# Decay factors of a selective scan in two sets of tiles, one bank of PSUM and two tiles of SBUF each, written two rounds ahead

## The chip, the core and the metric

The kernel runs on one core of a Trainium2 chip. The metric is the device time of one execution in microseconds: 8020.21 us, the median of three runs (8017.12 to 8021.32). The profile is of one further execution.

## What is computed

The reference is a small hybrid network on images of 56 x 56 positions and 96 channels, in float32, four of them in a batch: two state-space blocks, each with a selective scan in four directions, and then two layers of linear attention with a quantised feed-forward net. The two scans take nearly all of the time. Cut to what matters here, one direction of one image is

```
dt  = softplus(dt_raw @ dtw.T + dtb)                 # 192 channels, 3136 positions
d_a = exp(dt[..., None] * a)                         # 192 channels x 16 states
d_b = dt[..., None] * b_ssm[:, None, :]
h_t = d_a_t * h_(t-1) + d_b_t * x_t                  # the recurrence over positions
y_t = sum over states of h_t * c_t
```

In this text d_a is called the decay, d_b times x the product, and the sum over states is y. There are 2 blocks x 4 images x 4 directions = 32 such scans.

## The kernel before

The 3136 positions of a direction are cut into 7 steps of 448 (`CS`). The 192 x 16 pairs of channel and state of one step are cut into 8 rounds: two halves of the channels (e) and four groups of states (q). A round has 3 groups (g) of 128 partitions, each partition one pair of channel and state. So there are 32 x 7 x 8 = 1792 rounds.

The engines take a round between them as follows; the lines are those of the profile.

- TensorE spreads the round's rows of B over 128 partitions into the PSUM tile b (line 616, `spread_b`, called from `begin`).
- ScalarE writes the three decays of the round, exp of dt times a, to the tiles da0, da1 and da2 (line 678, `decay`).
- VectorE multiplies du (dt times the input) by b for g = 0 and 1 (line 719, `products`), into the tile h. GpSimd does the same for g = 2 from its own copy of B in SBUF, cb (line 714).
- VectorE runs the recurrence of each g in place in h with the decay tile as the factor (line 726, `scan`).
- GpSimd multiplies the three groups of h by C, also in cb, into hc (line 768).
- Two rounds later TensorE sums hc over the states into the PSUM tile y (line 799), and ScalarE moves y out after each fourth round (line 806).

Before, da0 to da2 are three PSUM tiles of one bank each, with a single set: the decay of round n+1 is written to a tile as soon as the scan of round n has read it. [...]

A step is prepared over the rounds ahead of it, at offsets o counted in rounds from its first round: parameters and inputs (o = -14 and -12), projection on TensorE into pp (-12, -11), its rows to cf on ScalarE and the removal of the upper bits (-10 to -8), the step size dt with softplus (-8 to -6), the product du on GpSimd (line 521, o = -5), writing both to DRAM and reading them back spread over the partitions (lines 526 and 532, o = -5 to 0), and one read of cb for each q (line 550, o = -3 to 0). All these transfers are issued by SyncE's queue (SP).

Beside the scans, the other layers (`load`, `middle`, `branch`, `fuse`, `attend`) run as lanes: generators that give their instructions piece by piece at two places of a round, "F" (after the products) and "C" (between the scans of g = 0 and g = 1), while a budget of ScalarE and TensorE time (`spend`, `half_round`, `room`) lets them. Within the scan phase the order of the instructions on TensorE, ScalarE, VectorE and GpSimd is the order in which this program writes them, and each engine takes them in that order. `keep_busy` adds matmuls with zeros where TensorE would have little work in a round. After the last round, `late` gives the PSUM banks of the scans to the remaining lanes.

In the lanes, the convolution is done with matmuls by diagonal weights (dg), built by GpSimd (line 932, 27 small instructions) when the first image reaches it. Windows of the image for it lie in `win` with `NWIN` buffers.

Of the kernel before, what the change touches and what calls it, by code (L numbers as in the profile page):

```python
# [11 lines left out]
F32 = mybir.dt.float32  # L12
# [3 lines left out]
AF = mybir.ActivationFunctionType  # L16
ALU = mybir.AluOpType
# [5 lines left out]
C = 96  # L23
# [3 lines left out]
NG = 3  # L27
NQ = 4
NT = 112
CW = 448  # L30
# [6 lines left out]
NCS = L // CS  # L37
RANK = (12, 6)
NW, LATE_NW = 13, 20
NWIN = 5  # L40
OWN = ()
OWN_TAIL = ()

# [124 lines left out]
class Net:  # L168
    def __init__(self, ctx, tc, aps, at, out):
        self.tc, self.nc, self.aps, self.at, self.out = tc, tc.nc, aps, at, out  # L170
        pool = lambda name, **kw: ctx.enter_context(tc.tile_pool(name=name, **kw))
        self.const = pool("const", bufs=1)
        self.big = pool("big", bufs=1)
        self.psum = pool("psum", bufs=1, space=bass.MemoryType.PSUM)
        self.dram = pool("dram", bufs=1, space=bass.MemoryType.DRAM)
        self.nw, self.nwin, self.depth, self.banks, self.ring = NW, NWIN, DEPTH, BANKS, None
        self.tables = False
        self.both = self.big.tile([C, NE, L], F32, name="U")
        self.U = [self.both[:, e] for e in range(NE)]
        self.Y = [self.big.tile([C, L], F32, name=f"Y{e}") for e in range(NE)]  # L180
        self.wp = pool("work", bufs=2)
        self.setup()
        self.dg = None
        self.kept = (0, 0, 0)
        self.ready, self.loaded = set(), set()
        self.live, self.g = [], {}
        self.backlog, self.paced = [0.0, 0.0], False
        self.work = 0.0
        self.pool = pool
        d = lambda name, *shape: [self.dram.tile(list(shape), F32, name=f"{name}{i}") for i in range(NB)]  # L190
        self.ud, self.zd, self.yd, self.xrd = d("u", DI, L), d("z", DI, L), d("y", DI, L), d("xr", C, L)
        self.fd = d("f", C, L)
        self.xw, self.mw = d("x", C, L + 2 * HS), d("m", DI, L + 2 * HS)
        self.xd, self.md = [[t[:, HS : HS + L] for t in a] for a in (self.xw, self.mw)]
# [6 lines left out]
    def late(self):  # L201

        self.scan_pool.close()
        self.wp = self.pool("late", bufs=2)
        self.nw, self.nwin, self.depth, self.banks = LATE_NW, LATE_DEPTH + 1, LATE_DEPTH, LATE_BANKS
        tags = (("ps", BANKS), ("da0", 1), ("da1", 1), ("da2", 1), ("pp", 1), ("b", 1), ("y", 1))
        self.ring = cycle([t for t in tags for _ in range(t[1])])

    def ps(self):
# [345 lines left out]
    def prepare(self, ch, o):  # L555

        nc = self.nc
        if o == -14:  # L560
            self.parameters(ch)
        if o == (-14 if ch.opening else -12):
            self.inputs(ch)
        if o == -9:
            ch.cd = self.dram.tile([2 * NS, CS], F32, tag="cd", name="cd", bufs=3)
            nc.sync.dma_start(ch.cd, ch.cf[: 2 * NS])
        elif o == -5:
            self.times_u(ch)
            ch.dtd = self.park(ch.dtc)
        elif o == -4:  # L570
            ch.dud = self.park(ch.duc)
            self.spread_dt(ch, 0)
        elif o == -3:
            self.spread_du(ch, 0)
        elif o == 0:
            self.spread_du(ch, 1)
            self.spread_dt(ch, 1)
        if -3 <= o <= 0:
            self.fetch(ch, o + 3)

    def prepare_on_scalar(self, ch, o):

        if o == -10:
            self.rows(ch)
        elif o in (-9, -8):
            part = slice(64 if o == -9 else 96, 128)
            self.nc.scalar.copy(ch.cf[part], ch.ps[part])  # L587
        elif o in (-7, -6):
            self.softplus(ch, o + 7)

    def on_tensor(self, ch, o):

        for e in self.projected(ch, o):
            self.project_step(ch, e)
        if o in (-10, -9):
            self.less(ch, 64 if o == -10 else 96)
        elif o in (-8, -7):
            self.step_size(ch, o + 8)

    def projected(self, ch, o):  # L600

        return () if o not in (-12, -11) else (o + 12,) if not ch.first else (0, 1) if o == -11 else ()

    def less(self, ch, at):

# [6 lines left out]

    def spread_b(self, ch, q):

        ps = self.psum.tile([128, 512], F32, tag="b", name="b", bufs=1)[:, :CS]
        self.nc.tensor.matmul(ps, self.sel[:, q], self.upper(ch.cf), start=True, stop=True)  # L616
        return ps

# [4 lines left out]
    def scans(self):  # L623
# [24 lines left out]
        per = NE * NQ  # L648


        da = [self.psum.tile([128, 512], F32, name=f"da{g}")[:, : CS + 4] for g in range(NG)]
        for t in da:
            nc.vector.memset(t, 0.0)

        def steps(n):
# [4 lines left out]
            for ch, o in steps(n):  # L660
                self.on_tensor(ch, o)

        for n in range(-14, 0):
            for ch, o in steps(n):
                self.prepare(ch, o)
            if n > -8:
                yield "F", n, 0
            for ch, o in steps(n):
                self.prepare_on_scalar(ch, o)
            ahead(n)  # L670
            if n > -8:
                yield "C", n, 0

        def decay(n, g):

            if n < len(rounds):
                ch, e, q = rounds[n]
                nc.scalar.activation(da[g][:, INNER], ch.dt[e][:, g], AF.Exp, scale=ch.par.na[:, e, q, g : g + 1])  # L678

        def column(t, at):  # L680

# [39 lines left out]
        def scan(n, g):  # L721
            ch, e, q = rounds[n]
            c = 1 if ch.step else 0
            way = slice(CS + 1 + c, 1, -1) if ch.rev else slice(2 - c, CS + 2)
            h = hs[n][:, g * ROW :]
            nc.vector.tensor_tensor_scan(h[:, way], da[g][:, way], h[:, way], 0.0, ALU.mult, ALU.add)  # L726

        carried(0)
        carried(1)
        begin(0)  # L730
        self.exp_and_ln()
        self.tables = True
        for g in range(NG):
            decay(0, g)
        late = []
        for n, (ch, e, q) in enumerate(rounds):
            r = NQ * e + q
            products(n)
            for c, o in steps(n):
                self.prepare(c, o)  # L740
            self.half_round()
            strided = [1.5 + 1.5 * ch.orient] * (r % NQ == 2)
            strided += [1.5 + 1.5 * c.orient for c, o in steps(n) for _ in self.projected(c, o)]
            self.spend((0.6, 0.7, 1.7, 0, 0, 0, 0.7, 0.6)[r], (1.3, 1.3, 0, 0, 0, 0, 0.4, 0.4)[r] + sum(strided))
            yield "F", n, r
            for c, o in steps(n):
                self.prepare_on_scalar(c, o)
            ended = late.pop(0) if len(late) == 2 else None
            if ended:
                self.keep_busy(ended[2])  # L750
            begin(n + 1)
            if ended:
                self.add_up(*ended)
            ahead(n)
            self.half_round()
            for g in range(NG):
                if g == 1:
                    yield "C", n, r
                if g == 2 and ended and ended[2] == NQ - 1:
                    self.spend(0.6, 0)  # L760
                    self.keep_sums(*ended[:3])
                scan(n, g)
                if g == 2:
                    kept(n)
                decay(n + 1, g)
            carried(n + 2)
            hc = sp.tile([128, NG, CS], F32, name="hc", bufs=3)
            nc.gpsimd.tensor_tensor(  # L768
                hc, tokens(hs[n]), ch.cb[q][:, 0].unsqueeze(1).to_broadcast([128, NG, CS]), ALU.mult,
            )  # L770
            late.append((ch, e, q, hc))
            del hs[n], bs[n]
# [148 lines left out]
    def get(self, d, rows, s):  # L921
        t = self.w(rows)
        self.nc.sync.dma_start(t, d[:, s])
        return t

    def diagonals(self, w):

        t = self.wp.tile([C, 3 * NG, 3, 32], F32, name="dg", bufs=1)
        out = []
        for n in range(w.shape[1] // 3):  # L930
            for x in range(3):
                self.nc.gpsimd.tensor_scalar_mul(t[:, n, x], self.three, w[:, 3 * n + x : 3 * n + x + 1])
                yield "F0"
            out.append(t[:, n])
        return out

    def conv(self, diag, parts):
# [98 lines left out]
    def middle(self, i):  # L1036
# [49 lines left out]

        yield from self.overlap(part, NCW)

        if self.dg is None:
            self.dg = yield from self.run(self.diagonals(par("c96", "1conv_w")))  # L1090
        dg = self.dg

        def convolve(c):
# [212 lines left out]
    def gram(self, n, i, c, x, s):  # L1306

        nc = self.nc
        xr = self.wp.tile([C + 1, CW], F32, name="xra", bufs=self.depth)
        nc.scalar.activation(xr[C:], self.ident[C : C + 1, :1].to_broadcast([1, CW]), AF.Copy, scale=0.0, bias=1.0)  # L1310
        yield from self.normed(1e-5, x, 1, xr[:C])
        nc.sync.dma_start(self.xrd[i][:, s], xr[:C])
# [60 lines left out]
def tile_net(ctx: ExitStack, tc: tile.TileContext, aps, at, out):  # L1373
# [12 lines left out]
    lanes = alone([net.load(0)], lambda: "normed" in net.loaded)  # L1386
    net.fold_weights()
    net.open_scans()
    lanes = alone(lanes, lambda: 1 in net.loaded)

    beside = [
# [40 lines left out]
```

## Time and profile before

| | |
|---|---|
| median of 3 runs | 8020.21 us |
| profiled execution | 8016.8 us |
| its span | 8014.9 us |
| VectorE (DVE) busy | 7522.8 us, 94% |
| GpSimd (POOL) busy | 7170.8 us, 89% |
| TensorE (PE) busy | 7013.7 us, 88% |
| ScalarE (ACT) busy | 6114.5 us, 76% |
| first product to end of last scan | 87.17 to 7810.39 us |
| granted TensorE clock, mean | 0.907 |

A group of instructions is given as line, engine, operation, the tiles out<-in, the shape and the count, then the busy time in us and the mean of one in ns, then the idle time of that engine right before these instructions, and which instruction of another engine ended it. In a timeline the first two numbers are the start and the length in us; instructions of one kind that follow one another are merged (x2, x3). An engine that is blocked inside an instruction counts as busy.

### The profile page before, as it was taken

The page shows a single profiled execution, that of the slowest core. Times are in us where ns is not written, and L with a number is a line of the kernel's source. Part 1 is how long each engine was busy: PE and PEld are TensorE (multiplying, and loading weights), DVE is VectorE, ACT ScalarE, POOL GpSimd, SP SyncE. Part 2 cuts the span into 40 slices and gives each one's busy share as a digit, 9 for nine tenths or more (in the row PEclk, how much of TensorE's full clock was granted, in tenths as well). Part 3 has the DMA queues.
Part 4 walks back from the last instruction along what each step waited for, and adds up shares of the span by engine and source line. Part 5 has one row for each costly group of instructions (what it writes and reads, how often), then busy time and mean ns, then how long its engine had stood idle before and what let it go on. Part 6 is the DMA issues. An engine that isn't in the chain of part 4 may idle for free.

```text
span 8014.9 us, 113446 instructions
## 1 busy us (share of the span) xinstructions
PE 7013.7 (88%) x33765; PEld 2326.8 (29%) x33765; DVE 7522.8 (94%) x9600; ACT 6114.5 (76%) x12759; POOL 7170.8 (89%) x3989
## 2 busy tenths in 40 slices
PE   7888888889888988899889988988889888898888
PEld 3222222222222222222222223322233222332224
DVE  6999999999999999999999999999999999999992
ACT  6778878777778768887678876787877877678776
POOL 5999999999999999999989998999989999899990
PEclk8889989989899989999889999988999999998998
DMA  5556655557555665566655666555565555655552
GB/s 180 181 188 191 197 186 187 173 188 228 186 182 180 222 199 186 170 196 203 196 182 172 195 212 202 180 163 167 185 203 170 167 172 191 192 172 169 174 171 70
DMA packets 568239, 1467.53 MB, mean 183 GB/s; under 512 B 108034, under 2 KB 337156, under 8 KB 566756
## 3 DMA queue, kind: packets, MB, share of 16 engines
q1 hardware_dynamic: 566848, 1458.49, 57.0%
q8 instruction: 265, 4.34, 0.2%
q14 instruction: 354, 2.90, 0.1%
q10 hardware_dynamic: 772, 1.80, 0.1%
HBM read 1186.49 MB, written 273.47 MB: 182 GB/s over the span
## 4 chain that ended last, share of the span: by engine, by line
DVE 32%; PE 31%; ACT 17%; issue 13%; POOL 4%; DMA 2%; DVEq 0%; SPq 0%; POOLq 0%; ACTq 0%
DVE h L726 23%; DVE h L719 7%; PE y L799 6%; ACT da L678 5%; PE y L786 5%; PE y L795 4%; PE b L616 3%; POOL hc L768 2%; PE pp L496 2%; ACT L830 2%; PE ps L947 2%; PE pp L448 1%; ACT Y L806 1%; PE ps L863 1%; PE ps L824 1%
## 5 line engine op out<-in xcount | busy, mean ns | idle before, releaser
L726 DVE TENSOR_TENSOR_SCAN h<-da,h 128x449 f32<-128x449 f32 (+1 forms) x5376 | 5510.3, 1073 | 98.4 <-ACT da L678 82.6
L768 POOL TENSOR_TENSOR hc<-h,cb 128x1344 f32<-128x1344 f32 x1792 | 4887.1, 2727 | 539.7 <-DVE h L726 431.4
L678 ACT ACTIVATE da<-dt,na 128x448 f32<-128x448 f32 x5376 | 3353.7, 632 | 1077.1 <-DVE h L726 1053.3
L719 DVE TENSOR_TENSOR h<-du,b 128x448 f32<-128x448 f32 x3584 | 2019.9, 605 | 96.5 <-PE b L616 62.2
L799 PE MATMUL y<-hc,four 128*32 128x448 f32 x14336 | 1916.1, 610 | 16.0 <-POOL hc L768 15.9
L714 POOL TENSOR_TENSOR h<-du,cb 128x448 f32<-128x448 f32 x1792 | 1756.1, 980 | 46.0 <-ACT h L691 26.3
L786 PE MATMUL y<-w,zeros 128*96 128x448 bf16 x5143 | 1433.0, 397 | 0.0
L616 PE MATMUL b<-cf,sel 128*128 128x448 bf16 x1792 | 672.4, 375 | 731.7 <-DVE h L719 726.7
L786 PEld LDWEIGHTS <-zeros 128*96 128x96 bf16 x5143 | 635.6, 134 | 1177.4 <-issue 1017.9
L448 PE MATMUL pp<-U,wd 96*128 96x448 f32 x896 | 662.6, 828 | 10.9 <-DMA U<-u 5.6
L799 PEld LDWEIGHTS y<-hc,four 128*32 128x32 f32 x14336 | 294.5, 113 | 1232.2 <-issue 719.3
L795 PE MATMUL y<-Y,ident 96*96 96x448 f32 x672 | 537.5, 889 | 35.7 <-ACT Y L806 20.2
L496 PE MATMUL pp<-cf,wd 12*96 12x448 f32 (+1 forms) x896 | 477.9, 615 | 98.3 <-ACT dtc L506 51.9
L521 POOL TENSOR_TENSOR duc<-dtc,U 96x896 f32<-96x896 f32 x224 | 483.3, 2157 | 27.0 <-ACT dtc L508 27.0
L696 ACT COPY carry<-h 128x3 f32<-128x3 f32 x1536 | 302.0, 197 | 263.4 <-DVE h L726 257.6
L806 ACT COPY Y<-y 96x448 f32<-96x448 f32 x448 | 341.7, 763 | 28.2 <-PE y L799 27.2
L691 ACT COPY h<-carry 128x3 f32<-128x3 f32 x1536 | 280.0, 182 | 48.2 <-POOL hc L768 44.9
L587 ACT COPY cf<-pp 64x448 f32<-64x448 f32 x448 | 235.8, 526 | 87.6 <-PE pp L609 79.3
L506 ACT ACTIVATE dtc<-pp,wd 96x448 f32<-96x448 f32 x448 | 281.8, 629 | 17.6 <-PE pp L496 13.3
L616 PEld LDWEIGHTS <-sel 128*128 128x128 bf16 x1792 | 179.0, 100 | 367.3 <-issue 296.7
L496 PEld LDWEIGHTS pp<-cf,wd 12*96 12x96 f32 (+1 forms) x896 | 113.6, 165 | 468.5 <-ACT dtc L506 175.6
L863 PEld LDWEIGHTS ps<-rsb,ident 128*96 128x96 f32 x1768 | 207.3, 178 | 126.3 <-issue 77.6
(383 smaller groups left out, 5392.7 us busy)
## 6 DMA issues: line engine op xcount, KB each, us to landing
cb<-cd SPq DMA_DIRECT2D x896, 448.0 KB, 4.8
dt<-dd SPq DMA_DIRECT2D x448, 672.0 KB, 5.8
du<-dd SPq DMA_DIRECT2D x448, 672.0 KB, 5.5
dd<-dtc SPq DMA_DIRECT2D x672, 112.0 KB, 2.0
dd<-duc SPq DMA_DIRECT2D x672, 112.0 KB, 2.0
win<-m SPq DMA_DIRECT2D x252, 112.0 KB, 4.3
U<-u SPq DMA_DIRECT2D x112, 168.0 KB, 4.8
w<-z SPq DMA_DIRECT2D x84, 224.0 KB, 4.1
```

The lines of the kernel that those rows point to most:

```text
L448: self.nc.tensor.matmul(ch.ps.rearrange("p (a b) -> p a b", b=HS), ch.par.wx[:, e], self.in_order(self.U[e], ch.orient, ch.c * CS, CS), st ...
L496: self.nc.tensor.matmul(ch.pd, ch.par.wt[rows, C * e : C * e + C], ch.cf[rows], start=True, stop=True)
L521: self.nc.gpsimd.tensor_tensor(in_rows(ch.duc), in_rows(ch.dtc), u[:, :, lo : lo + CS // HS], ALU.mult)
L616: self.nc.tensor.matmul(ps, self.sel[:, q], self.upper(ch.cf), start=True, stop=True)
L678: nc.scalar.activation(da[g][:, INNER], ch.dt[e][:, g], AF.Exp, scale=ch.par.na[:, e, q, g : g + 1])
L714: nc.gpsimd.tensor_tensor(tokens(hs[n])[:, 2], ch.du[e][:, 2], ch.cb[q][:, 1], ALU.mult)
L719: nc.vector.tensor_tensor(tokens(hs[n])[:, g], ch.du[e][:, g], bs[n], ALU.mult)
L726: nc.vector.tensor_tensor_scan(h[:, way], da[g][:, way], h[:, way], 0.0, ALU.mult, ALU.add)
L768: nc.gpsimd.tensor_tensor(hc, tokens(hs[n]), ch.cb[q][:, 0].unsqueeze(1).to_broadcast([128, NG, CS]), ALU.mult,)
L786: self.nc.tensor.matmul(self.y[:C], self.zeros[:, :C], self.some, start=False, stop=False)
L795: nc.tensor.matmul(o, w, self.in_order(a, ch.orient, ch.c * CS, CS), start=True, stop=False)
L799: nc.tensor.matmul(self.y[32 * n : 32 * n + 32], self.four, hc[:, g], start=n == 3, stop=n == 3 or q == NQ - 1,)
```

## The change

The decays get two sets of tiles. In each set g = 0 has a PSUM bank and g = 1 and 2 have a tile of SBUF each; round n uses set n mod 2. The decays of round n+2 are written behind the scans of round n, those of rounds 0 and 1 before the first round. The bank of PSUM that comes free (three da banks become two) is a second one for b. Each part of a step's preparation up to the first spread is one round sooner, and so is the read of the second half of dt; the second half of du and cb stay where they are. The estimates in `spend` are moved along by a round.

To make room in SBUF, `NWIN` is 4 in place of 5, and the diagonals no longer have a tile of their own: they lie in three of the tiles that the attention layers later use as xra. They are built once, before the scans begin.

```diff
-NWIN = 5
+NWIN = 4
...
-        tags = (("ps", BANKS), ("da0", 1), ("da1", 1), ("da2", 1), ("pp", 1), ("b", 1), ("y", 1))
+        tags = (("ps", BANKS), ("da0", 1), ("da1", 1), ("pp", 1), ("b", 2), ("y", 1))
...
-        if o == -14:
+        if o == -15:
             self.parameters(ch)
-        if o == (-14 if ch.opening else -12):
+        if o == (-15 if ch.opening else -13):
             self.inputs(ch)
-        if o == -9:
+        if o == -10:
             ch.cd = self.dram.tile([2 * NS, CS], F32, tag="cd", name="cd", bufs=3)
             nc.sync.dma_start(ch.cd, ch.cf[: 2 * NS])
-        elif o == -5:
+        elif o == -6:
             self.times_u(ch)
             ch.dtd = self.park(ch.dtc)
-        elif o == -4:
+        elif o == -5:
             ch.dud = self.park(ch.duc)
             self.spread_dt(ch, 0)
-        elif o == -3:
+        elif o == -4:
             self.spread_du(ch, 0)
+        elif o == -1:
+            self.spread_dt(ch, 1)
         elif o == 0:
             self.spread_du(ch, 1)
-            self.spread_dt(ch, 1)
...
-        ps = self.psum.tile([128, 512], F32, tag="b", name="b", bufs=1)[:, :CS]
+        ps = self.psum.tile([128, 512], F32, tag="b", name="b", bufs=2)[:, :CS]
...
-        da = [self.psum.tile([128, 512], F32, name=f"da{g}")[:, : CS + 4] for g in range(NG)]
-        for t in da:
+        da = [
+            [
+                self.psum.tile([128, 512], F32, name=f"da{s}")[:, : CS + 4] if g == 0
+                else sp.tile([128, CS + 4], F32, name=f"da{s}{g}", bufs=1)
+                for g in range(NG)
+            ]
+            for s in range(2)
+        ]
+        for t in chain(*da):
             nc.vector.memset(t, 0.0)
...
-                nc.scalar.activation(da[g][:, INNER], ch.dt[e][:, g], AF.Exp, scale=ch.par.na[:, e, q, g : g + 1])
+                nc.scalar.activation(da[n % 2][g][:, INNER], ch.dt[e][:, g], AF.Exp, scale=ch.par.na[:, e, q, g : g + 1])
...
-            nc.vector.tensor_tensor_scan(h[:, way], da[g][:, way], h[:, way], 0.0, ALU.mult, ALU.add)
+            nc.vector.tensor_tensor_scan(h[:, way], da[n % 2][g][:, way], h[:, way], 0.0, ALU.mult, ALU.add)
...
-        for g in range(NG):
-            decay(0, g)
+        for n in range(2):
+            for g in range(NG):
+                decay(n, g)
...
-            self.spend((0.6, 0.7, 1.7, 0, 0, 0, 0.7, 0.6)[r], (1.3, 1.3, 0, 0, 0, 0, 0.4, 0.4)[r] + sum(strided))
+            self.spend((0.7, 1.7, 0, 0, 0, 0.7, 0.6, 0.6)[r], (1.3, 0, 0, 0, 0, 0.4, 0.4, 1.3)[r] + sum(strided))
...
-                decay(n + 1, g)
+                decay(n + 2, g)
...
+    def wide_row(self):
+        return self.wp.tile([C + 1, CW], F32, name="xra", bufs=self.depth)
+
     def diagonals(self, w):
 
-        t = self.wp.tile([C, 3 * NG, 3, 32], F32, name="dg", bufs=1)
         out = []
         for n in range(w.shape[1] // 3):
+            if n % 4 == 0:
+                t = self.wide_row()[:C, : 4 * C].rearrange("p (n x k) -> p n x k", n=4, k=32)
             for x in range(3):
-                self.nc.gpsimd.tensor_scalar_mul(t[:, n, x], self.three, w[:, 3 * n + x : 3 * n + x + 1])
-                yield "F0"
-            out.append(t[:, n])
+                self.nc.gpsimd.tensor_scalar_mul(t[:, n % 4, x], self.three, w[:, 3 * n + x : 3 * n + x + 1])
+            out.append(t[:, n % 4])
         return out
...
     net.open_scans()
+    net.dg = net.diagonals(net.par("c96", "1conv_w"))
```

The same shift by one round is made in `prepare_on_scalar`, `on_tensor` and `projected`, and the prologue of the scans has 15 rounds in place of 14.

## The prediction

> **What bounds the kernel now.** I read the busy shares first, then the groups of instructions, the table of waits, and last the timeline of a few rounds. The page, whose group lines end in busy time, mean ns of one, and the idle time ahead of them:
>
> ```profile
> ## 1 busy us (share of the span) xinstructions
> PE 7013.7 (88%) x33765; PEld 2326.8 (29%) x33765; DVE 7522.8 (94%) x9600; ACT 6114.5 (76%) x12759; POOL 7170.8 (89%) x3989
> ...
> L726 DVE TENSOR_TENSOR_SCAN h<-da,h 128x449 f32<-128x449 f32 (+1 forms) x5376 | 5510.3, 1073 | 98.4 <-ACT da L678 82.6
> L768 POOL TENSOR_TENSOR hc<-h,cb 128x1344 f32<-128x1344 f32 x1792 | 4887.1, 2727 | 539.7 <-DVE h L726 431.4
> L678 ACT ACTIVATE da<-dt,na 128x448 f32<-128x448 f32 x5376 | 3353.7, 632 | 1077.1 <-DVE h L726 1053.3
> L719 DVE TENSOR_TENSOR h<-du,b 128x448 f32<-128x448 f32 x3584 | 2019.9, 605 | 96.5 <-PE b L616 62.2
> ...
> L714 POOL TENSOR_TENSOR h<-du,cb 128x448 f32<-128x448 f32 x1792 | 1756.1, 980 | 46.0 <-ACT h L691 26.3
> ```
>
> VectorE is the bound at 94%, and GpSimd stands close behind at 89%. A round is two products (L719), three scans (L726), one GpSimd product (L714) and one GpSimd multiplication by C (L768); there are 1792 rounds. The timeline of the last rounds has products starting at 7798.28, 7802.29 and 7806.30: an undisturbed round is 4.01 us, all VectorE. Rounds run from 87.17 to 7810.39 us, 7723 us or 4.31 each, and what lies around them is 8014.9 - 7723.2 = 292 us.
>
> The waits (us, times, longest) are what the change can remove:
>
> ```profile
> ACT da L678 <- DVE h L726: 1053.3, 1754, 4.0
> ...
> PE b L616 <- DVE h L719: 726.7, 784, 2.7
> ...
> POOL hc L768 <- DVE h L726: 431.4, 726, 6.0
> ...
> DVE h L726 <- ACT da L678: 82.6, 175, 1.9
> ...
> DVE h L719 <- PE b L616: 62.2, 72, 9.6
> ```
>
> The first two are idle time of engines that aren't the bound. VectorE itself waits 82.6 + 5.5 us for decays and 62.2 us for B, of which 9.6 is the first round. In the table by stage VectorE is idle for 280 us of the scan phase in all.
>
> Now what overlaps what (start, length):
>
> ```profile
> 4000.21 1.13 DVE L719 TENSOR_TENSOR h<-du,b 128x448 f32<-128x448 f32 x2
> ...
> 4000.43 2.71 POOL L768 TENSOR_TENSOR hc<-h,cb 128x1344 f32<-128x1344 f32 x1 [0.36 <-DVE h L726]
> ...
> 4001.25 3.05 DVE L726 TENSOR_TENSOR_SCAN h<-da,h 128x449 f32<-128x449 f32 x3
> ...
> 4003.11 1.76 POOL L521 TENSOR_TENSOR duc<-dtc,U 96x896 f32<-96x896 f32 x1
> ...
> 4004.84 0.97 POOL L714 TENSOR_TENSOR h<-du,cb 128x448 f32<-128x448 f32 x1
> ```
>
> All three scans run under GpSimd work and take their usual time. Every large VectorE instruction here has one operand in PSUM: da in the scans, b in the products. GpSimd reads both of its inputs from SBUF.
>
> **What the Trainium skill says.** "SBUF — State Buffer", section "Who interferes with whom": VectorE has one SBUF read port of its own and one that it shares with GpSimd; with at most one SBUF input it doesn't contend, but "A DVE instruction with two SBUF inputs contends with a GpSimd instruction that reads SBUF", and the lock is exclusive for the whole instruction. The trace agrees with the first half (scans of 1055 to 1094 ns throughout). No two-SBUF-input instruction meets GpSimd here. The lock itself, though, can be seen in the tail, where L1258 (SBUF to SBUF, a form that the same section lists as taking both ports) twice starts inside a GpSimd instruction. VectorE, then GpSimd:
>
> ```profile
> 7897.47 0.34 DVE L1258 TENSOR_SCALAR h<-h,b1q 128x448 f16<-128x448 f16 x1
> ...
> 7898.93 0.78 DVE L1258 TENSOR_SCALAR h<-h,b1q 128x448 f16<-128x448 f16 x1
> ```
>
> ```profile
> 7898.54 1.03 POOL L1286 TENSOR_TENSOR w<-w,yq 96x448 f32<-96x448 f32 x1 [33.84 <-ACT yq L1284]
> ```
>
> GpSimd ends at 7899.57, VectorE at 7899.71: 0.78 us for an instruction of 0.34, ended 0.14 after the release. The other instance (7974.37, 0.83 us) ends 0.13 after GpSimd.
>
> "ScalarE: Activation LUTs", in "Step-by-step: what each stage is for", says that ScalarE writes PSUM faster than SBUF. Rows: 632 ns for da into PSUM, 666 ns for L1216, SBUF to SBUF.
>
> **The change part by part.**
>
> *Two of three decays in SBUF.* Scans g=1 and g=2 now read da and h, both from SBUF, and so need the shared port; g=0 doesn't. Per round GpSimd is busy 3.98 us (7139.5 us in the scan phase by stage / 1792: 2.73 + 0.98, L521 every eighth round, some lane work), and all of it reads SBUF. If the lock holds, these 3.98 us and the two scans exclude each other. In order: hc ends, and GpSimd's next product follows it at once (in the timeline GpSimd's instructions start 0.03 before the last ends); scan g=1, waiting, ends between 0.87 (0.14 + 1.07 - 0.34, as with L1258) and 1.07 + 0.14 = 1.21 us after the release; scan g=2 follows 0.99 later (three take 3.05); 0.14 later hc starts (4000.29 to 4000.43). That is 2.00 to 2.34 us in which GpSimd stands. The products, scan g=0 and lane work of VectorE, about 2.3 us, lie under hc. A round is 3.98 + 2.00 to 2.34 = 5.98 to 6.32 us; I take 6.2. If GpSimd's product slips in between the two scans, two more handovers of 0.14 make it up to 6.6. 1792 x 6.2 = 11110; with 292 around it, 11402. Without a lock the cost is nothing: SBUF as source is no slower by the nearest rows (L280, both SBUF, 96x96: 0.24 us; L1351, one in PSUM: 0.242).
>
> *ScalarE writing to SBUF.* 34 ns x 3584 = 122 us of ScalarE work, under the 1053 us that it waits for VectorE; even without that cover it has 24% free.
>
> *Decays two rounds ahead.* Removes at most the 88 us; the write waits for the scan two rounds back, done a round earlier. ScalarE's other queue (carries, cf, softplus) shifts with it. Behind the lock this gain vanishes, since VectorE then waits for the port.
>
> *Two banks for B.* Removes up to 52.6 us of VectorE's wait and TensorE's 726.7 us, which bound nothing.
>
> *A step's preparation a round sooner.* No instruction added. On SP's queue one dt transfer per step (672 KB, 5.8 us to landing) moves ahead of a du and a cb; cd, dd and the first spreads keep their order. L521 moves a round on GpSimd's queue. 7.2 us of VectorE's waits are for du: bound -7 to +50 us, under a longer round nothing. Four window buffers in place of five can hold SP behind TensorE's reading; hidden likewise.
>
> *Diagonals at the start.* 27 x 386 ns = 10.4 us leave the scan phase's GpSimd queue and stand ahead of L871 at the head: 8 to 18.4 us, where L871 began at 12.92. At most +5.5 us; VectorE's L889 behind that first L871 (17.38) waited for nothing, so I take +3. The 15th prologue round adds no work.
>
> Sum on the profiled execution's span: 11402 + 3 = 11405. Its own time was 8016.8, and the median of the runs 8020.2, 5 us over the span: 11,400.
>
> **The rivals.**
> *No lock for scans (faster).* A scan takes an element only every second cycle by its 1073 ns against 605 for a product, so GpSimd may find the port free. Then 8014.9 - 88 - 52.6 + 3 = 7877: about 7,880, between 7,740 (all 280 us of idle gone) and 8,010. For: no trace here shows a two-input instruction blocked. Against: the skill's sentence and L1258. It decides where both scans together lose under 0.08 us a round (141 / 1792).
> *The port shared word by word.* GpSimd reads 3584 words per partition in 3.71 us, 1.035 ns each; 898 more for the scans make 0.93 us, so 4.91 us a round, GpSimd the bound: 1792 x 4.91 + 292 = 9,090, between 8,300 and 9,400. Against: L1258 waited to the end.
> *Lock, and TensorE slows too.* The skill's "TensorE: Matmul & The Clock Gate", Part 1, halves the clock after an idle window of about 3.4 us; the page shows 0.8 to 0.9. TensorE has some 3.8 us of work in 6.2; cold, up to twice that in part, so up to 6.8 us a round and 12,500.
>
> **How the numbers follow.** Lock 0.64 (11,000 to 12,150); lock with slips or a cold TensorE 0.10 (to 12,500); shared port 0.10; no lock 0.16, of which 0.13 faster, 0.01 the same, 0.02 slower. Faster 0.13, same 0.01, slower 0.86. The bound for these is 0.2%, 16 us, about what a measurement tells from no change. The lock's own range is 10,900 to 12,400 and holds 0.73; to reach 0.8 the range must take in most of the shared port: 8,600 to 12,400.
>
> **What would show it.** In the profile after: scans of g=1 and g=2 in a group of their own with a mean well over 1073 ns, or GpSimd's L768 and L714 lengthened, with a blocked instruction counted as busy; no overlap of these scans with GpSimd's instructions in the timeline; scans of g=0 still at 1.07; VectorE's waits for da and b gone; rounds of some 6.2 us. I am wrong if the SBUF scans stay at 1.07 us over running GpSimd instructions of 2.73 us, or if the GpSimd instructions only stretch by some 0.5 us.

## The result and the profile after

The changed kernel takes 10820.08 us (median of four runs, 10819.06 to 10821.02) against 8018.66 us of the kernel before beside it: a ratio of 1.3502, 95% interval 1.3486 to 1.3518. The forecast was 11,400, slower, with a range of 8,600 to 12,400.

The page of the changed kernel, in the columns of the one before:

```profile
PE 8032.5 (74%) x33718; PEld 2568.1 (24%) x33718; DVE 10558.8 (98%) x9609; ACT 6285.2 (58%) x12754; POOL 8669.3 (80%) x3989
...
L733 DVE TENSOR_TENSOR_SCAN h<-da,h 128x449 f32<-128x449 f32 (+1 forms) x5376 | 8569.3, 1640 | 0.0
L776 POOL TENSOR_TENSOR hc<-h,cb 128x1344 f32<-128x1344 f32 x1792 | 4873.0, 2719 | 1883.7 <-DVE h L733 1647.5
L685 ACT ACTIVATE da<-dt,na 128x448 f32<-128x448 f32 x5376 | 3520.4, 657 | 2911.8 <-DVE h L733 2893.0
L721 POOL TENSOR_TENSOR h<-du,cb 128x448 f32<-128x448 f32 x1792 | 2994.2, 1671 | 0.5 <-ACT h L698 0.5
...
L726 DVE TENSOR_TENSOR h<-du,b 128x448 f32<-128x448 f32 x3584 | 2006.4, 599 | 13.0 <-PE b L616 12.9
```

A scan grew from a mean of 1073 to 1640 ns, GpSimd's product (L721) from 980 to 1671 and its product du from 2157 to 2941, while the products of VectorE and the multiplication by C kept their length. No wait of VectorE shows any of this: the idle time before the scans is 0.0. GpSimd's wait for the scans ahead of hc, 431 us before, is 1647.5. A blocked instruction counts as busy, so VectorE looks fuller (98%) and only its mean betrays it. 5376 scans x 567 ns are 3048 us, more than the whole loss of 2801.

One round of the changed kernel in the timeline, VectorE and GpSimd lines of it:

```profile
5004.27 2.73 POOL L776 TENSOR_TENSOR hc<-h,cb 128x1344 f32<-128x1344 f32 x1 [1.09 <-DVE h L733]
...
5005.10 4.57 DVE L733 TENSOR_TENSOR_SCAN h<-da,h 128x448 f32<-128x448 f32 x3
...
5006.96 1.76 POOL L721 TENSOR_TENSOR h<-du,cb 128x448 f32<-128x448 f32 x1
...
5009.59 1.12 DVE L726 TENSOR_TENSOR h<-du,b 128x448 f32<-128x448 f32 x2
...
5009.81 2.72 POOL L776 TENSOR_TENSOR hc<-h,cb 128x1344 f32<-128x1344 f32 x1 [1.09 <-DVE h L733]
```

Three scans take 4.57 us in place of 3.05. The product of GpSimd starts where hc ends and takes 1.76 us for work of 0.98: it stands 0.78 us behind the scan of g=1. Then it ends at 5008.72, and the last scan only at 5009.67, 0.95 later. The two engines alternate: hc, a scan, the product, a scan. The round is 5.54 us.

Not every round goes so. Two rounds later, VectorE and then GpSimd:

```profile
5017.72 5.34 DVE L733 TENSOR_TENSOR_SCAN h<-da,h 128x448 f32<-128x448 f32 x3
```

```profile
5017.49 2.71 POOL L776 TENSOR_TENSOR hc<-h,cb 128x1344 f32<-128x1344 f32 x1
5020.16 0.97 POOL L721 TENSOR_TENSOR h<-du,cb 128x448 f32<-128x448 f32 x1
5023.21 2.73 POOL L776 TENSOR_TENSOR hc<-h,cb 128x1344 f32<-128x1344 f32 x1 [2.08 <-PE pp L447]
```

The scan of g=1 has stood since the one of g=0 ended near 5018.8, and hc ends at 5020.20. Yet the product goes first and takes no more than its usual time; both scans follow it, to 5023.06. By a count over the trace, 261 of the 3231 scans that stood were passed by a further GpSimd instruction in this way.

The first rounds of VectorE in the same kernel show both cases:

```profile
95.61 3.05 DVE L733 TENSOR_TENSOR_SCAN h<-da,h 128x448 f32<-128x448 f32 x3
...
99.62 4.51 DVE L733 TENSOR_TENSOR_SCAN h<-da,h 128x448 f32<-128x448 f32 x3
```

```profile
89.50 1.91 POOL L721 TENSOR_TENSOR h<-du,cb 128x448 f32<-128x448 f32 x2
98.74 2.72 POOL L776 TENSOR_TENSOR hc<-h,cb 128x1344 f32<-128x1344 f32 x1 [7.33 <-DVE h L733]
```

In the first round GpSimd (the second block) runs nothing from 91.41 to 98.74, and three scans, two of them with both inputs in SBUF, take 3.05 us as ever. In the second they run beside hc and take 4.51.

### The profile page after: what moved, and what is told of

Read it like the earlier page. It is cut to its first block, busy times and chain, and to the rows that moved or that the text cites. A ratio compares the mean times of both kernels' runs of the same rounds, so it can differ in the third digit from the quotient of the medians.

```text
span 10817.3 us, 110232 instructions
## 1 busy us (share of the span) xinstructions
PE 8032.5 (74%) x33718; PEld 2568.1 (24%) x33718; DVE 10558.8 (98%) x9609; ACT 6285.2 (58%) x12754; POOL 8669.3 (80%) x3989
## 3 DMA queue, kind: packets, MB, share of 16 engines
q14 instruction: 332, 2.72, 0.1%
## 5 line engine op out<-in xcount | busy, mean ns | idle before, releaser
L733 DVE TENSOR_TENSOR_SCAN h<-da,h 128x449 f32<-128x449 f32 (+1 forms) x5376 | 8569.3, 1640 | 0.0
L776 POOL TENSOR_TENSOR hc<-h,cb 128x1344 f32<-128x1344 f32 x1792 | 4873.0, 2719 | 1883.7 <-DVE h L733 1647.5
L685 ACT ACTIVATE da<-dt,na 128x448 f32<-128x448 f32 x5376 | 3520.4, 657 | 2911.8 <-DVE h L733 2893.0
L721 POOL TENSOR_TENSOR h<-du,cb 128x448 f32<-128x448 f32 x1792 | 2994.2, 1671 | 0.5 <-ACT h L698 0.5
L807 PE MATMUL y<-hc,four 128*32 128x448 f32 x14336 | 2150.4, 679 | 259.0 <-POOL hc L776 257.6
L726 DVE TENSOR_TENSOR h<-du,b 128x448 f32<-128x448 f32 x3584 | 2006.4, 599 | 13.0 <-PE b L616 12.9
L794 PE MATMUL y<-w,zeros 128*96 128x448 bf16 x5096 | 1660.4, 450 | 0.0
L520 POOL TENSOR_TENSOR duc<-dtc,U 96x896 f32<-96x896 f32 x224 | 658.9, 2941 | 22.5 <-ACT dtc L507 22.5
L609 PE MATMUL pp<-cf,minus 64*64 64x448 bf16 x448 | 199.1, 444 | 571.7 <-ACT cf L490 289.3
L803 PEld LDWEIGHTS y<-Y,ident 96*96 96x96 f32 x672 | 122.9, 228 | 855.5 <-ACT Y L814 809.4
L832 PE MATMUL ps<-w,cen 96*96 96x448 f32 x466 | 266.1, 669 | 70.3 <-DVE w L1250 14.7
L871 PE MATMUL ps<-rsb,ident 128*96 128x112 f32 x1800 | 285.5, 317 | 44.1 <-ACT rsb L866 30.4
```

The lines of the kernel that those rows point to most:

```text
L520: self.nc.gpsimd.tensor_tensor(in_rows(ch.duc), in_rows(ch.dtc), u[:, :, lo : lo + CS // HS], ALU.mult)
L685: nc.scalar.activation(da[n % 2][g][:, INNER], ch.dt[e][:, g], AF.Exp, scale=ch.par.na[:, e, q, g : g + 1])
L721: nc.gpsimd.tensor_tensor(tokens(hs[n])[:, 2], ch.du[e][:, 2], ch.cb[q][:, 1], ALU.mult)
L726: nc.vector.tensor_tensor(tokens(hs[n])[:, g], ch.du[e][:, g], bs[n], ALU.mult)
L733: nc.vector.tensor_tensor_scan(h[:, way], da[n % 2][g][:, way], h[:, way], 0.0, ALU.mult, ALU.add)
L776: nc.gpsimd.tensor_tensor(hc, tokens(hs[n]), ch.cb[q][:, 0].unsqueeze(1).to_broadcast([128, NG, CS]), ALU.mult,)
```

## The experiments

The theory is the lock: a scan with both inputs in SBUF and a GpSimd instruction that reads SBUF exclude each other. The rivals are that other parts of the change cost the time (moved transfers, two rounds of distance that hold ScalarE's queue), and that such a scan is slow by itself.

**The rest of the change alone.**

```diff
 (the changed kernel)
-        da = [[... PSUM for g == 0, SBUF for g = 1, 2 ...] for s in range(2)]
+        da = [self.psum.tile([128, 512], F32, name=f"da{g}")[:, : CS + 4] for g in range(NG)]
...
-                decay(n + 2, g)
+                decay(n + 1, g)
...
-        ps = self.psum.tile([128, 512], F32, tag="b", name="b", bufs=2)[:, :CS]
+        ps = self.psum.tile([128, 512], F32, tag="b", name="b", bufs=1)[:, :CS]
```

> The changed kernel with the decays as before (three PSUM banks, one set, one round ahead) and one bank for B; the earlier preparation, the four windows and the early diagonals stay. Lock theory: the two SBUF decays carry all of the loss, so this stands within 50 us of 8,020. Rival, the moved transfers or the fewer windows hold SP's queue up: near 10,800.

Measured: 8014.46 us, ratio 0.9999 (0.9991 to 1.0008). The earlier preparation, four windows and early diagonals together make no difference that can be measured. The next three runs differ from this kernel in the decay tiles only.

**Decays in SBUF, one set, one round ahead: g=1 and g=2, g=2 alone, g=0 alone.**

```diff
+            sp.tile([128, CS + 4], F32, name=f"sd{g}", bufs=1) if g in (1, 2)   # (2,) and (0,) in the others
+            else self.psum.tile([128, 512], F32, name=f"da{g}")[:, : CS + 4]
```

> As the run with the rest of the change alone, but the decays of g=1 and g=2 lie in SBUF, in a single set and one round ahead. Lock theory: the set and the distance don't matter, 10,600 to 11,000 with the two SBUF scans at a mean near 1.9 us. Rival, writing two rounds ahead blocks ScalarE's queue (it waits 2893 us for scans in the changed kernel): back to within 50 us of 8,020.

Measured: 10807.49 us, ratio 1.3483 (1.3458 to 1.3508): the whole loss, without the second set, the second bank and the distance. VectorE's groups of this run tell the scans apart by their decay tile (sd in SBUF, da in PSUM):

```profile
L730 DVE TENSOR_TENSOR_SCAN h<-sd,h 128x449 f32<-128x449 f32 (+1 forms) x3584 | 6707.4, 1910 | 0.0
...
L730 DVE TENSOR_TENSOR_SCAN h<-da,h 128x449 f32<-128x449 f32 (+1 forms) x1792 | 1931.6, 1078 | 1.1 <-ACT da L682 1.1
```

Only the scans with two inputs in SBUF are longer. Writing two rounds ahead isn't what costs the time, since the loss is whole with one.

> Only the decay of g=2 in SBUF, one set. Lock theory: hc 2.72, GpSimd's product 0.98, then the scan of g=2 with 0.95 and 0.14 to the next hc, 4.76 us a round, with 0.3 for the other GpSimd work 5.05: 9,340, from 9,100 to 9,500. Rival, a scan with both inputs in SBUF is slow by itself (the three scans of the changed kernel take 1.72 us more a round, 0.86 each): 4.31 + 0.86 = 5.17 a round, 9,560.

Measured: 9348.06 us, 1.1662 (1.1641 to 1.1684). The scans with their decay in SBUF are the group

```profile
L730 DVE TENSOR_TENSOR_SCAN h<-sd,h 128x449 f32<-128x449 f32 (+1 forms) x1792 | 3416.2, 1906 | 8.0 <-POOL h L718 6.0 <-ACT h L695 1.7
```

and those with it in PSUM have a mean of 1070 ns. A regular round, VectorE's scan of g=2 and then GpSimd:

```profile
5047.18 1.81 DVE L730 TENSOR_TENSOR_SCAN h<-sd,h 128x449 f32<-128x449 f32 x1
```

```profile
5044.37 2.73 POOL L772 TENSOR_TENSOR hc<-h,cb 128x1344 f32<-128x1344 f32 x1 [1.09 <-DVE h L730]
5047.06 0.98 POOL L718 TENSOR_TENSOR h<-du,cb 128x448 f32<-128x448 f32 x1
5049.13 2.73 POOL L772 TENSOR_TENSOR hc<-h,cb 128x1344 f32<-128x1344 f32 x1 [1.09 <-PE y L790]
```

Here the sum of the lock holds in its parts: hc, the product, the scan that ends 0.95 us behind it, and the next hc 0.14 later are 4.76 us. That is also the median of all rounds; the mean is 5.04, where 5.05 was expected. Rounds in which GpSimd makes du (line 520) are longer, up to 6.9 us (5017.64 to 5024.53).

> Only the decay of g=0 in SBUF, one set. Lock theory: this scan wants to start 1.05 us after the last one ended, under hc, and must wait for hc's end; the scans of g=1 and g=2 stand behind it: 0.14 + 2.69 + 0.9 + 1.98 = 5.7 us a round, 10,300 to 10,700, slower than with g=2 in SBUF by about 1,000. Rival, slow by itself: the place doesn't matter, 9,560 as with g=2.

Measured: 11173.63 us, 1.3940 (1.3914 to 1.3965). Groups of VectorE in this run:

```profile
L730 DVE TENSOR_TENSOR_SCAN h<-sd,h 128x449 f32<-128x449 f32 (+1 forms) x1792 | 5385.0, 3005 | 2.4 <-ACT sd L682 2.4
L730 DVE TENSOR_TENSOR_SCAN h<-da,h 128x449 f32<-128x449 f32 (+1 forms) x3584 | 3664.9, 1060 | 0.0
```

The same one scan with the same two inputs takes 1906 ns at g=2 and 3005 ns at g=0. A scan that was slow by itself would not care about its place; this rival falls. One such scan at g=0 costs even more than two at g=1 and 2: it waits for the end of hc, and the other two stand behind it, so that none of the three runs beside hc. The size missed its range, 10,300 to 10,700. The regular round is 5.78 us by the median, near the 5.7 expected (two scans start at 5000.81 and 5006.58), but I had let du hide in GpSimd's idle time. The round behind a du takes 6.9 (5034.45 to 5041.36): there the scan stands from 5035.50, and hc, starting at 5035.78 behind GpSimd's product, still goes first. By a count over the trace such rounds lose 254 us against the regular one, and rounds in which VectorE also works for the other layers 207.

**GpSimd's multiplication by C cut short, before and after the change.** The rest of hc, in three fixed tiles, is zeroed once.

```diff
-                hc, tokens(hs[n]), ch.cb[q][:, 0].unsqueeze(1).to_broadcast([128, NG, CS]), ALU.mult,
+                hc[:, :, :16], tokens(hs[n])[:, :, :16], ch.cb[q][:, 0, :16].unsqueeze(1).to_broadcast([128, NG, 16]), ALU.mult,
```

> The kernel before with GpSimd's multiplication by C cut from 448 to 16 columns of each group (hc 128x48; the rest of hc stays zero, so y is left incomplete). VectorE stays the bound: 7,960 to 8,020 by every theory.

> The changed kernel with the same cut of GpSimd's multiplication by C (y is left incomplete). Lock theory: with hc gone from under the scans they meet only GpSimd's product and the product du, so the scans return to a mean near 1.1 us and the time to 7,750 to 8,050; what the two sets and two banks are worth without the lock shows against the kernel before with the same cut, 141 us by the sum of the prediction. Rival, scans with both inputs in SBUF are slow by themselves: the mean stays at 1.64 us and the time near 10,800.

Measured: 7963.92 us before (0.9928 of the kernel before, 0.9912 to 0.9944) and 8231.31 us after (1.0255, 1.0232 to 1.0277). Without hc under the scans the loss shrinks from 2801 to 267 us, but the time stays above the range I gave, 7,750 to 8,050. The mean scan is 1129 ns. The timeline of VectorE and then of GpSimd in the changed kernel with the short multiplication shows what is left:

```profile
5005.36 3.04 DVE L737 TENSOR_TENSOR_SCAN h<-da,h 128x448 f32<-128x448 f32 x3
...
5009.37 3.85 DVE L737 TENSOR_TENSOR_SCAN h<-da,h 128x448 f32<-128x448 f32 x3
```

```profile
5004.77 0.98 POOL L725 TENSOR_TENSOR h<-du,cb 128x448 f32<-128x448 f32 x1
...
5008.78 1.76 POOL L520 TENSOR_TENSOR duc<-dtc,U 96x896 f32<-96x896 f32 x1
5010.51 1.76 POOL L725 TENSOR_TENSOR h<-du,cb 128x448 f32<-128x448 f32 x1
```

The product ends before the SBUF scans begin, except in the round with du: du ends at 5010.54, in the time of the second scan, and the product behind it again waits 0.78 us. By a count over the two traces, rounds with du and those right behind them make some 180 of the 258 us by which the rounds are longer than before; the others share the rest.

**Memsets in place of the multiplication by C.**

```diff
-            nc.gpsimd.tensor_tensor(hc, tokens(hs[n]), ch.cb[q]..., ALU.mult)
+            nc.gpsimd.memset(hc, 0.0)
+            nc.gpsimd.memset(hc, 0.0)
```

> The changed kernel with GpSimd's multiplication by C replaced by two memsets of hc, which read nothing (y is left out: zero). Lock on reads only: the scans of g=1 and g=2 meet only the reads of the product and of du, as in the run with the short multiplication, under 8,200. Lock on any GpSimd access: the memsets, some 1.2 us each, hold the scans, over 9,500.

Measured: 8253.82 us, 1.0290 (1.0266 to 1.0314), a little above the 8,200. The two memsets keep GpSimd nearly as long as the real multiplication (2.43 us against 2.72), but they only write. VectorE and then GpSimd:

```profile
5007.95 3.05 DVE L733 TENSOR_TENSOR_SCAN h<-da,h 128x449 f32<-128x449 f32 x3
```

```profile
5008.36 1.22 POOL L776 MEMSET hc<- 128x1344 f32 x1
5009.64 1.22 POOL L777 MEMSET hc<- 128x1344 f32 x1
```

Three scans run over two memsets, and none of the five is longer than alone. A GpSimd instruction that only writes doesn't hold these scans, so the lock is on its reads. The reads tried all belong to instructions with two inputs in SBUF; GpSimd instructions with one input were not tried in the rounds.

**No reads by GpSimd in the scan steps, before and after the change.**

```diff
-                nc.gpsimd.tensor_tensor(tokens(hs[n])[:, 2], ch.du[e][:, 2], ch.cb[q][:, 1], ALU.mult)
+                nc.gpsimd.memset(tokens(hs[n])[:, 2], 0.0)
...                                                  (hc and duc likewise)
```

> The kernel before with GpSimd's work of the scan steps replaced by memsets that read nothing (hc, the product of g=2 and du are zero, so y is left out). VectorE stays the bound by every theory: 7,930 to 8,000.

> The changed kernel with the same replacement (y is left out). Lock on reads: no read of GpSimd but the few of the lanes is left, the mean of the scans is 1.06 to 1.08 us with both inputs in SBUF, and what two sets and two banks are worth without the lock shows against the kernel before with the same replacement: 141 us less by the sum of the prediction, 70 to 200. If the short-multiplication run's remaining 0.06 us a scan was not the lock but the form, the mean stays at 1.13.

Measured: 7960.96 us before (0.9932, 0.9917 to 0.9947) and 7954.00 us after (0.9919, 0.9899 to 0.9938). The scans are back at a mean of 1073 ns with two inputs in SBUF:

```profile
L733 DVE TENSOR_TENSOR_SCAN h<-da,h 128x449 f32<-128x449 f32 (+1 forms) x5376 | 5516.9, 1073 | 1.8 <-POOL h L721 1.8
```

That is what the lock asks for. But two sets and two banks are worth 7 us here, within the intervals, and not 141. Where the gain went is in the waits. VectorE's largest before and after:

```profile
DVE h L726 <- ACT da L678: 76.5, 177, 1.9
DVE h L719 <- PE b L616: 61.2, 76, 9.6
```

```profile
DVE h L726 <- PE b L616: 105.5, 92, 11.9
```

And TensorE's before and after:

```profile
PE b L616 <- DVE h L719: 750.0, 801, 2.6
```

```profile
PE y L801 <- ACT Y L812: 252.0, 172, 3.2
PE y L801 <- ACT carry L703: 243.7, 159, 4.0
PE pp L609 <- ACT cf L490: 143.5, 74, 5.2
```

VectorE's waits for decays are all but gone, as the change means. Summed by releaser, VectorE waits 148 us for ScalarE before and 62 after, but 260 us for TensorE before and 333 after; the totals are 422 and 417. TensorE no longer waits for a bank of B; it now waits for ScalarE at other matmuls (y, pp), and B is no earlier for it. That ScalarE's order, with its decays further ahead, makes these waits was not tried apart.

**One input in SBUF per scan, and the control for it.**

```diff
 (the changed kernel; the control is the kernel before with the first two, and start in its scan)
-                nc.scalar.copy(column(hs[n], ROW if ch.rev else 1), ch.par.carry[:, e, q])
+            start = ch.par.carry[:, e, q, g : g + 1] if ch.step else 0.0     # the scan's initial value
...
-            nc.vector.tensor_tensor_scan(h[:, way], da[n % 2][g][:, way], h[:, way], 0.0, ALU.mult, ALU.add)
+            nc.vector.tensor_tensor_scan(h[:, way], da[n % 2][g][:, way], (h if g == 2 else pr[g])[:, way], start, ALU.mult, ALU.add)
```

> The changed kernel, but each scan has one input in SBUF: the decays of g=0 and g=1 stay in two sets in SBUF, two rounds ahead, and the products of these groups are written by VectorE to two PSUM banks; g=2 keeps a PSUM decay in one set and its product in SBUF; one bank for B; the state at a step's start comes in as the scan's initial value, so ScalarE's 1536 copies of 128x3 into h go. Lock theory: no scan meets the lock, the mean is 1.05 to 1.12 us and the time 7,850 to 8,020. Rival, decays in SBUF are what costs: over 9,000.

> The kernel before with only that last part: the state at a step's start as the scan's initial value in place of ScalarE's copies into h. It saves 1536 x 182 ns of ScalarE, part of it in the waits for decays: 7,950 to 8,020 if the initial value by pointer costs the scan nothing; each 10 ns that it costs adds 46 us over the 4608 scans that have one.

Measured: 8155.70 us (1.0171, 1.0151 to 1.0190) and, for the control, 8191.16 us (1.0221, 1.0203 to 1.0239): both above their ranges. VectorE's scans with products in PSUM (pr), then those of the control:

```profile
L731 DVE TENSOR_TENSOR_SCAN h<-da,carry,pr 128x448 f32<-128x448 f32 x3072 | 3374.2, 1130 | 0.0
...
L731 DVE TENSOR_TENSOR_SCAN h<-da,pr 128x448 f32<-128x448 f32 x512 | 532.0, 1070 | 0.0
```

```profile
L726 DVE TENSOR_TENSOR_SCAN h<-da,carry,h 128x448 f32<-128x448 f32 x4608 | 4987.1, 1129 | 37.9 <-ACT da L678 25.8 <-POOL h L714 5.3 <-issue 0.2
...
L726 DVE TENSOR_TENSOR_SCAN h<-da,h 128x448 f32<-128x448 f32 x768 | 784.6, 1068 | 16.1 <-ACT da L678 13.3 <-POOL h L714 2.8
```

The run also writes these products to PSUM (pr) and has one bank for B. Decays in SBUF cost nothing when the other input is in PSUM: 1130 against 1129 ns, over a GpSimd that multiplies as ever (2728 ns). What both pay is the initial value by pointer, 61 ns a scan, 4608 x 61 = 281 us. The control, which spares ScalarE's copies, is 175 us slower than the kernel before. The initial value was my own addition, and it hides what the version could have been; against the control the version gains 35 us. A version that keeps the state's column, with products in PSUM, was not run, and none of the runs on the whole computation is faster than the kernel before.

**One bank for B in the changed kernel.**

```diff
-        ps = self.psum.tile([128, 512], F32, tag="b", name="b", bufs=2)[:, :CS]
+        ps = self.psum.tile([128, 512], F32, tag="b", name="b", bufs=1)[:, :CS]
```

> The changed kernel with one bank for B in place of two. Lock theory: VectorE's wait for B hides behind the lock or adds at most what it was, so 10,800 to 10,900, and TensorE's wait for the products comes back to some 700 us. If the second bank does something that the lock doesn't hide, over 10,900.

Measured: 10830.76 us, 1.3503 (1.3483 to 1.3523), the same ratio as with two banks. TensorE's wait for the products is 2450.6 us, not some 700, and costs nothing that shows: VectorE waits 20.6 us for B in all.

## Why the prediction was right, and where it was off

**The bound and the lock.** Right. The sentence of the Trainium skill on two SBUF inputs ("SBUF — State Buffer", section "Who interferes with whom"), which the trace before couldn't show for such an instruction, holds here: a scan that GpSimd held up ends 0.95 us after GpSimd's instruction, inside the 0.87 to 1.21 that were worked out from L1258. Rounds with and without a running GpSimd, PSUM against SBUF in one kernel, the place of the scan, and memsets against reads each show it apart.

**The size.** 5% too high, and the term is the time that GpSimd stands per round. I had it at 2.00 to 2.34 us, with the product right behind hc and both scans after it. Where the engines do go in that order, as at 5020.16, GpSimd stands 2.08 us, so that price was right. But in most rounds they alternate. I took that to be dearer, up to 6.6 us a round, and it is cheaper: the product stands 0.78, and from its end the last scan and the handover take 0.95 + 0.14, so 1.87 us in all. With 3.98 that is 5.85 us, and the measured mean is 5.86 (94.55 to 10600.62 us, 1792 rounds); I used 6.2. The rounds took 10,506 us where 11,110 were forecast, 604 less. Around them lie 311 us where 295 were forecast, 16 more: 7 at the head, where I had put 3 for the diagonals, and the rest behind the last scan. Together this is the gap of 588 between the forecast span and 10817.3.

**The range.** 10,820 lies below the lock's own range, 10,900 to 12,400. The range that was forecast holds it because it was taken down to 8,600 for the sake of a rival that fell. As far as the size goes, that is luck: the lock's range alone would have missed by 80 us.

**ScalarE into SBUF.** 34 ns a decay were estimated; 670 ns in SBUF against 637 in PSUM are the medians of the run with the decay of g=0 in SBUF. Hidden, as said: the changed kernel's wait of VectorE for decays is 0.

**The waits removed.** VectorE's waits for decays and for B are gone, from 82.6 + 5.5 and 62.2 to 0 and 12.9, of which 11.95 is the first round. That this gain vanishes behind the lock was right.

**The faster rival.** Its mechanism fell: the scans did not find the port free. That a scan takes an element only every second cycle was read from 1073 against 605 ns, a ratio of 1.8, and no run shows it. Its size was wrong too. It took each of VectorE's waits as time to be had (141 us). With GpSimd's reads out of the way the same edits gave 7. The failed step is the subtraction of 88 and 52.6 us from the span: another wait, TensorE's, came last in their place.

**The other rivals.** The port is not shared word by word: a scan that stands ends 0.95 us after GpSimd's instruction whatever that one's length, and 10,820 lies far over the 9,090 of that case. TensorE's granted clock did fall, from 0.907 to 0.789, and the y matmul went from 610 to 679 ns; but VectorE's wait for B was 12.9 us in all, and the lock alone accounts for the round. That the clock halves, no run here shows.

## What to carry to other kernels

Before a tile moves from PSUM to SBUF, count the SBUF inputs of each VectorE instruction that reads it: a second one made the scans here exclude GpSimd's instructions that read SBUF, and two engines at 94% and 89% have no room for that. The profile shows it as longer instructions, not as waits, so compare means of one instruction by form and by where its operands lie. A wait of the bounding engine is worth its length only if the next releaser isn't right behind it: here 86 us less of waits for ScalarE came with 73 us more for TensorE.

## What the runs showed that I had not expected

- In most rounds the lock goes from one engine to the other after each instruction: the product, which has stood since 5006.96, goes ahead of VectorE's next scan. In others GpSimd gets two instructions in a row past a scan that stands (5020.16 above). What decides between the two is not shown.
- A handover costs less than the lengths on the page add up to. In the round shown first the product ends at 5008.72, so its 0.98 us of work begins at about 5007.74; ScalarE's decay that waits for the scan of g=1 starts only at 5007.98. Whether the scan lets go before its record ends or GpSimd's instruction starts before it needs the lock, no run tells.
- The place of a locked instruction can matter more than the number: one locked scan at g=0 cost 11,174 us, two at g=1 and g=2 10,807.
- An initial value by pointer makes a scan 61 ns longer (1129 against 1068 ns).
